# A selective scan on one Trainium2 core: GpSimd's operand instruction made over two channel blocks, and one more weighing moved to GpSimd

## The chip, the core and the metric

One core of one Trainium2 (trn2) chip runs the whole program; the other cores are idle. The metric is device microseconds of the program (us), and smaller is better. A core has five engines that each run their own instruction stream in order: PE (TensorE, matmul and transpose), DVE (VectorE), ACT (ScalarE), POOL (GpSimd) and SP (SyncE, which here only issues DMAs). They wait for each other by semaphores. SBUF is the working memory, PSUM the small memory that PE writes its results to.

## What is computed

A layer with two parts. The first is a bidirectional selective scan (two Mamba blocks, forward and backward in time), the second a mixture of eight experts with two chosen per token plus a shared expert. The input x is 2 batches x 2048 tokens x 256 channels, all in float32. The change lies in the first part. Cut to what matters:

```python
def _mamba(x, W_in, W_conv, b_conv, W_x, W_dt, b_dt, A_log, Dp, W_out):
    xp, z = split(x @ W_in.T)                       # 512 inner channels each
    xc = silu(causal_depthwise_conv(xp) + b_conv)
    dt, Bm, Cm = split(xc @ W_x.T, [16, 32])        # Bm, Cm: 16 states each
    dt = softplus(dt @ W_dt.T + b_dt)
    A = -exp(A_log)                                 # 512 x 16
    def step(h, (dt_t, u_t, B_t, C_t)):             # over time
        h = h * exp(dt_t[:, :, None] * A) + (dt_t * u_t)[:, :, None] * B_t[:, None, :]
        return h, einsum('bdn,bn->bd', h, C_t)
    y = scan(step) + xc * Dp
    return (y * silu(z)) @ W_out.T
```

So for every channel d and state n there is a recurrence over time. Its decay is exp(dt[d] A[d,n]). Its operand is (dt u)[d] B[n]; that product is what the changed instruction computes. Its result h is weighed with C[n] and summed over the 16 states.

## The kernel before

**Tiles.** Time is cut into 16 chunks (2 directions x 2 batches x 4 pieces of 512 tokens), run one after the other. A chunk has 512 channels in four blocks d of 128 partitions, and 16 states in eight groups g of NG = 2. A **step** is one channel block with one state group: a tile of 128 partitions x 2 states x 512 tokens. The steps of a chunk run over pairs p of blocks (0,1 and 2,3), inside that over g, inside that over the two blocks of the pair, so a chunk has SPC = 32 steps k = 0..31. Even k is the even block of a pair and odd k the odd one; two neighbours share B and C. `s` counts steps over all chunks, 512 in all.

**What a step does.**
- `load_b`, `load_c`: SP broadcasts two rows of B and of C to 128 partitions (3 and 4 buffers).
- `inputs` (L452): POOL multiplies du = dt u by B into `db`, one instruction of 128x1024 to a step. `db` has NDB = 10 buffers of one step.
- `decays` (L471): ACT writes the two decays `da` into PSUM banks that alternate between even and odd steps.
- `scans` (L485): DVE runs two scan instructions of 128x512.
- `weigh_own` (L491): DVE multiplies h by C, two instructions of 128x512; or, for the steps that `on_pool` names, `weigh` (L496): POOL does it in one instruction of 128x1024. For POOL the scan writes h to an SBUF tile `h` of 3 buffers, otherwise in place to PSUM.
- `carry` (L502, L506): ACT keeps the last column of h for the next chunk.
- `sums` (L518): PE transposes the weighed tile and adds it up in PSUM.
- `gate_y` (L536): after step 15 and step 31, DVE multiplies the sum by the gate.

In chunks 1 to 15 four **turned** steps (k = 6, 7, 18, 19) get their operand from PE instead of POOL; their `db` buffer holds the decay. `on_pool` names, in these chunks, the odd steps except k = 13 and 29, and also k = 4 and 16: sixteen of 32.

**The order is written out by hand.** The scheduler is off (`manual_schedule`), so each engine runs its instructions in the order in which the code emits them. In iteration s of the loop at L843 the order is: `load_b` (even s), `weigh(s-2)`, `load_c` (even s), `inputs(s+3)`, `carry(s-1)`, a softplus part at k = 20, 22, 24 and 26, `gate_y(s-5)`, `scans(s)`, `weigh_own(s)`, `decays(s+1)`, the turned operands of s+1, then the PSUM evacuations left over from the step before, `sums(s-4)`, and at last `visit(i, k)`. The last one places pieces of the neighbouring chunks' other work at fixed k (L545 to L569). Those that matter below: at k = 10 and 12 `scaled` (transposes that ACT evacuates at L372), at k = 11 `project` (evacuated by DVE at L421), at k = 12 `silu_inner` of the next chunk (L278, ACT: table load, 128x2048 silu, table load L212), at k = 13 and 15 `gated`, at k = 14 `dbc` of the next chunk (PE L289, evacuated by ACT at L294). These pieces share two PSUM banks (tag "mm"), so a third one waits until the first is evacuated. `du` itself (L342, POOL, 128x512) is made at k = 21, 23 and, in the next chunk, k = 0, 2.

Before the loop the same `db` buffers hold the input x and its normalised copy (`load_x`, `norms`).

Of the kernel before, what the change touches and what calls it, by code (L numbers as in the profile page):

```python
# [8 lines left out]
F32 = mybir.dt.float32  # L9
AF = mybir.ActivationFunctionType  # L10
ALU = mybir.AluOpType
# [4 lines left out]
P = 128  # L16
NB, T, C = 2, 2048, 256
# [6 lines left out]
TC = 512  # L24
NTC = T // TC
JC = TC // P
NG = 2
NGR = NS // NG
# [12 lines left out]
def kernel(  # L41
# [4 lines left out]
    nc = tc.nc  # L46
# [11 lines left out]
        out=flip, in_=flip, compare_op=ALU.not_equal, fill=1.0,  # L58
# [17 lines left out]
    def bc(ap, n):  # L76

        return ap.unsqueeze(1).to_broadcast([ap.shape[0], n, ap.shape[1]])

    def tiled(ap):  # L80

        return ap.rearrange("(j p) c -> p j c", p=P)
# [51 lines left out]
    with tc.tile_pool(name="mw", bufs=1) as mw, tc.tile_pool(name="mw2", bufs=2) as mw2, \  # L134
# [36 lines left out]
        def make_conv(r, n):  # L171

            w, (d, k) = weights[r], divmod(n, 4)
            if n == 0:
# [4 lines left out]
        weights, state, ready, xns, accs = {}, {}, {}, {}, {}  # L179
        chunks = [(r, b, t) for r in range(2) for b in range(NB) for t in range(NTC)]  # L180
        NCH = len(chunks)
        SPC = NP * NGR * 2
        steps = [(i, p, g, 2 * p + e) for i in range(NCH) for p in range(NP) for g in range(NGR)
                 for e in range(2)]
        NST = len(steps)
        NDB = 10
# [3 lines left out]
        def turned_step(s):  # L190
            i, p, g, _ = steps[s]
            return i > 0 and g == TURNED[p]

        def on_pool(s):

            i, _, g, d = steps[s]
            if i == 0:
                return d % 2 == 1 and g not in (NGR - 4, NGR - 2)
            return s % SPC in (4, 16) or d % 2 == 1 and g != NGR - 2

        def tokens(r, t):
            return t if r == 0 else NTC - 1 - t
# [227 lines left out]
        live = {}  # L430
# [15 lines left out]
            live["C", n] = v  # L446

        def inputs(s):
            i, _, g, d = steps[s]
            db = m2.tile([P, NG, TC], F32, tag="db", bufs=NDB, name=f"db{s}")  # L450
            if not turned_step(s):
                nc.gpsimd.tensor_tensor(db, bc(ready[i]["du"][:, d, :], NG), live["B", s // 2], ALU.mult)  # L452
            live["db", s] = db

        def operands(s):

# [36 lines left out]
        def weigh(s):  # L493
            _, _, g, d = steps[s]
            if on_pool(s):
                nc.gpsimd.tensor_tensor(live["db", s], live.pop(("h", s)), live["C", s // 2], ALU.mult)  # L496
# [107 lines left out]
        def new_stats(name):  # L604
            return {k: m2.tile([P, JC, n], F32, tag=f"n_{k}", name=f"{k}_{name}")
                    for k, n in (("st", 6), ("mv", 2), ("ve", 1), ("y", 1), ("t", 1), ("mr", 1))}

        def stats(v, src):
            for j in range(JC):
                nc.vector.bn_stats(out=v["st"][:, j, :], in_=src[:, j, :])  # L610
                nc.vector.bn_aggr(out=v["mv"][:, j, :], in_=v["st"][:, j, :])

        def rsqrt_start(v):

            y = v["y"].rearrange("p j o -> p (j o)")
            nc.scalar.activation(y, v["mv"][:, :, 1], AF.Ln, bias=eps)
            nc.scalar.activation(y, y, AF.Exp, scale=-0.5)

        def rsqrt_end(v):
            ve, y, t, mr = (v[k].rearrange("p j o -> p (j o)") for k in ("ve", "y", "t", "mr"))  # L620
            nc.vector.tensor_scalar(ve, v["mv"][:, :, 1], EPS, None, ALU.add)
            nc.vector.scalar_tensor_tensor(t, y, -0.5, y, ALU.mult, ALU.mult)
            nc.vector.tensor_tensor(t, t, ve, ALU.mult)
            nc.vector.scalar_tensor_tensor(y, t, 1.5, y, ALU.add, ALU.mult)
            nc.vector.scalar_tensor_tensor(mr, v["mv"][:, :, 0], -1.0, y, ALU.mult, ALU.mult)

        def normalize(out, v, src):
            for j in range(JC):
                nc.scalar.activation(out[:, j, :], src[:, j, :], AF.Identity,
                                     scale=v["y"][:, j, :], bias=v["mr"][:, j, :])  # L630

        def load_x(b, q):
            xt = m2.tile([P, JC, C], F32, tag="db", bufs=NDB, name=f"xt{b}_{q}")
            nc.sync.dma_start(out=xt, in_=tiled(x[b, q * TC:(q + 1) * TC, :]))
            return xt

        def norms(b, q, xt, xn):

            u = f"{b}_{q}"
            v = new_stats(f"a{u}")  # L640
            stats(v, xt)
            rsqrt_start(v)
            yield
            rsqrt_end(v)
            normalize(xt, v, xt)
            yield
            nc.vector.tensor_tensor(xt, xt, bc(mds[b][:, 1, :], JC), ALU.mult)
            nc.vector.tensor_tensor(xt, xt, bc(mds[b][:, 0, :], JC), ALU.add)
            nc.sync.dma_start(out=tiled(acc_d[b][q]), in_=xt)
            v = new_stats(f"b{u}")  # L650
            stats(v, xt)
            rsqrt_start(v)
            yield
            rsqrt_end(v)
            if xn is None:
                xn = m2.tile([P, JC, C], F32, tag="db", bufs=NDB, name=f"xo{u}")
            normalize(xn, v, xt)
            nc.sync.dma_start(out=tiled(xn_d[b][q]), in_=xn)

# [5 lines left out]
        xts = {(0, 0): load_x(0, 0)}  # L665
# [8 lines left out]
        make_rates(0)  # L674
        for n in range(4 * ND):
            make_conv(0, n)
        front = norms(0, 0, xts[0, 0], xns[0])
        next(front)
        next(front)
        for q in range(1, 3):  # L680
# [36 lines left out]
        def others():  # L717

            todo = [(0, 1), (0, 2), (0, 3), (1, 0), (1, 1)]
            live = []  # L720
            while todo or live:
                while todo and len(live) < 2:
                    k = todo.pop(0)
                    live.append(norms(*k, xts.pop(k), None))
                    if len(todo) > 1:
                        xts[todo[1]] = load_x(*todo[1])
                for g in list(live):
                    if next(g, 0) == 0:
                        live.remove(g)
                    yield  # L730
# [15 lines left out]
        for f, d in order:  # L746
            settle(False)
            e = f(0, d)
# [7 lines left out]
        for f, *d in ((dbc,), (delta, 0), (delta, 1), (delta, 2), (delta, 3)):  # L756
            settle(False)
            e = f(0, *d)
# [12 lines left out]
        for d in range(2):  # L771
            softplus_in(0, d, 1)
            softplus_out(0, d)
            input_(0, d)
        for s in range(3):
            inputs(s)
        decays(0)
        settle(False)
# [64 lines left out]
        for s in range(NST + 4 + SPC):  # L843
            i, k = divmod(s, SPC)
            if s % 2 == 0:
                if s // 2 + 3 < NST // 2:
                    load_b(s // 2 + 3)
            if 0 <= s - 2 < NST:
                weigh(s - 2)
            if s % 2 == 0 and s // 2 + 2 < NST // 2:  # L850
                load_c(s // 2 + 2)
            if s + 3 < NST:
                inputs(s + 3)
            smooth = (i + 1, soft[k]) if k in soft and i + 1 < NCH else None
            if i == 0 and k in first_soft:
                smooth = (0, first_soft[k])
            if 0 <= s - 1 < NST:
                carry(s - 1)
            if smooth:
                softplus_in(*smooth, s + 1)  # L860
                settle(False)
            if s == NST:
                open_front(0)
            if 0 <= s - 5 < NST:
                gate_y(s - 5)
            if s == NST + 5:
                open_front(0)
            if s < NST:
                scans(s)
            if smooth:  # L870
                softplus_out(*smooth)
            if s < NST:
                weigh_own(s)
            if s + 1 < NST:
                decays(s + 1)
                operands(s + 1)
            settle(False)
            settle(True)
            next(late, None)
            if 0 <= s - 4 < NST:  # L880
                sums(s - 4)
            if i == NCH - 1 and k in early_loads:
                early_loads[k][0](*early_loads[k][1:])
            if i == NCH and k in (10, 13, 14, 23):
                open_front({10: 0, 13: 1, 14: 0, 23: 1}[k])
            if i < NCH + 1:
                visit(i, k)
                if s == 8:
                    silu_gate(0)
                if k == 8 and 2 <= i < 2 + NB:  # L890
                    nc.sync.dma_start(out=xs_d[i - 2].rearrange("(p n) (m f) -> p (n m) f", p=P, f=P),
                                      in_=bc(ident, NTS * TS // P * 2))
            if i + 2 < NCH and chunks[i + 2][0] != chunks[i + 1][0]:
                r = chunks[i + 2][0]
                if k == 2:
                    fetch_weights(r)
                if 12 <= k < 12 + 4 * ND:
                    make_conv(r, k - 12)
                if k == 8:
                    make_rates(r)  # L900
                if k == 21:
                    fetch_dt(r)
                if k == 26:
                    fetch_in(r)
            if 0 < i < NCH and k == 24 and "out" not in weights[chunks[i][0]]:
                fetch_out(chunks[i][0])
# [500 lines left out]
```

## Time and profile before

Three runs gave a median of 2440.74 us (2439.56 to 2442.28). The profile comes from one further execution:

| what | value |
|---|---|
| the profiled execution's own time | 2438.82 us |
| its span, first to last instruction | 2436.9 us |
| mean granted TensorE clock | 0.895 of full |
| busy share: PE / DVE / ACT / POOL | 81% / 83% / 67% / 76% |
| POOL operands, L452 | 452 instructions, 2368 ns each |
| POOL weighing, L496 | 252 instructions, 2371 ns each |
| DVE scans, L485 | 1024 instructions in four groups, some 1.26 us each |
| DVE weighing, L491, h in `da` banks | 460 instructions, 676 ns each |

How to read it: a span of an instruction can overlap the next one's by some ten ns, so the sum over a row is a little above the time that the row takes; where it matters, the spacing from one start to the next is used. The loop over the chunks runs from about 105 us to 1896 us. The steady chunks (from about 760 us to 1780 us) repeat every 109.2 us: the first turned scan of a chunk starts at 1160.74, 1269.96, 1379.18, 1488.41 us. The expert part follows, from about 1900 us to the end, and is not touched.

### The profile page before, as it was taken

The page shows a single profiled execution, that of the slowest core. Times are in us where ns is not written, and L with a number is a line of the kernel's source. Part 1 is how long each engine was busy: PE and PEld are TensorE (multiplying, and loading weights), DVE is VectorE, ACT ScalarE, POOL GpSimd, SP SyncE. Part 2 cuts the span into 40 slices and gives each one's busy share as a digit, 9 for nine tenths or more (in the row PEclk, how much of TensorE's full clock was granted, in tenths as well). Part 3 has the DMA queues.
Part 4 walks back from the last instruction along what each step waited for, and adds up shares of the span by engine and source line. Part 5 has one row for each costly group of instructions (what it writes and reads, how often), then busy time and mean ns, then how long its engine had stood idle before and what let it go on. Part 6 is the DMA issues. An engine that isn't in the chain of part 4 may idle for free. (4 is left out here: it accounts for less than half of the span.)

```text
span 2436.9 us, 30322 instructions
## 1 busy us (share of the span) xinstructions
PE 1985.9 (81%) x9512; PEld 1369.4 (56%) x9512; DVE 2022.9 (83%) x2691; ACT 1621.1 (67%) x3375; POOL 1858.0 (76%) x979
## 2 busy tenths in 40 slices
PE   6366879797888878797888878797856698899997
PEld 2143545565655555565655545565546464788884
DVE  5499998999999999999999999999999675432333
ACT  5557786877778787877778787877765224354331
POOL 0367998989999999999999999999999205041305
PEclk9677888798989988898989988898977898999999
DMA  5344447484454454454454444444446312387873
GB/s 166 108 153 157 147 157 237 166 256 156 165 168 154 157 181 149 166 170 169 150 171 157 159 162 139 171 168 157 149 168 220 104 31 97 115 259 241 268 235 115
DMA packets 239974, 403.08 MB, mean 165 GB/s; under 512 B 38818, under 2 KB 171938, under 8 KB 239812
## 3 DMA queue, kind: packets, MB, share of 16 engines
q1 hardware_dynamic: 220724, 370.72, 46.5%
q0 software_dynamic: 6144, 16.79, 2.0%
q10 hardware_dynamic: 12944, 13.64, 1.6%
q8 instruction: 75, 1.23, 0.2%
q14 instruction: 87, 0.71, 0.1%
HBM read 346.54 MB, written 54.53 MB: 165 GB/s over the span
## 5 line engine op out<-in xcount | busy, mean ns | idle before, releaser
L452 POOL TENSOR_TENSOR db<-du,B 128x1024 f32<-128x1024 f32 x452 | 1061.5, 2368 | 14.2 <-DMA B<-bcs 14.1
L496 POOL TENSOR_TENSOR db<-h,C 128x1024 f32<-128x1024 f32 x252 | 597.5, 2371 | 67.5 <-issue 54.8
L471 ACT ACTIVATE da<-dt,w_a 128x512 f32<-128x512 f32 x904 | 594.7, 688 | 76.1 <-DVE dt L336 46.0
L518 PE MATMUL y<-ident,db 128*128 128x128 f32 x4096 | 570.1, 288 | 36.6 <-POOL db L496 34.0
L518 PEld LDWEIGHTS y<-ident,db 128*128 128x128 f32 x4096 | 506.6, 150 | 157.9 <-issue 102.1
L485 DVE TENSOR_TENSOR_SCAN da<-da,hl,db 128x512 f32<-128x512 f32 x460 | 562.9, 1269 | 4.9 <-POOL db L452 3.7
L485 DVE TENSOR_TENSOR_SCAN h<-da,hl,db 128x512 f32<-128x512 f32 x444 | 540.2, 1263 | 16.6 <-ACT da L471 16.4
L491 DVE TENSOR_TENSOR db<-da,C 128x512 f32<-128x512 f32 x460 | 292.2, 676 | 17.7 <-DMA C<-bcs 9.7
L272 PE MATMUL psc<-xp,w_conv 128*128 128x512 f32 x512 | 234.3, 601 | 9.4 <-ACT xp L261 6.4
L255 PE MATMUL psx<-xT,w_in 128*128 128x512 f32 x256 | 156.0, 730 | 100.2 <-ACT hl L506 86.8
L1104 POOL DMA_INDIRECT xs<-xs,slot x64 | 62.8, 981 | 203.5 <-ACT xs L1100 194.3
L390 PE MATMUL psz<-w_in,xT 128*128 128x512 f32 x256 | 149.3, 716 | 55.7 <-ACT bT L353 33.9
L1234 POOL DMA_INDIRECT two<-ys,slot x64 | 62.4, 974 | 159.7 <-DMA ys<-yo 64.3
L342 POOL TENSOR_TENSOR du<-dt,xc 128x512 f32<-128x512 f32 x64 | 81.5, 1274 | 98.9 <-DVE dt L336 98.9
L289 PE MATMUL psd<-xc,w_x 128*48 128x512 f32 x128 | 100.5, 959 | 67.5 <-ACT hl L506 47.6
L272 PEld LDWEIGHTS psc<-xp,w_conv 128*128 128x128 f32 x512 | 93.5, 192 | 106.7 <-issue 95.5
L418 PE MATMUL pso<-w_out,yg 128*128 128x256 f32 x512 | 118.5, 385 | 23.8 <-ACT e L312 22.6
L255 PEld LDWEIGHTS psx<-xT,w_in 128*128 128x128 f32 x256 | 50.0, 224 | 155.3 <-ACT hl L506 109.4
L1125 PE MATMUL pg<-fxT,s 128*128 128x512 f32 x256 | 120.1, 624 | 4.3 <-ACT hs L1130 4.0
L1180 DVE COPY gT<-qgT 128x512 f32<-128x512 f32 x46 | 31.8, 691 | 107.8 <-PE qgT L931 107.7
L506 ACT COPY hl<-da 128x1 f32<-128x1 f32 x460 | 61.7, 157 | 84.7 <-DVE db L491 82.1
L418 PEld LDWEIGHTS pso<-w_out,yg 128*128 128x128 f32 x512 | 95.6, 192 | 39.3 <-ACT e L312 25.6
(218 smaller groups left out, 3154.1 us busy)
## 6 DMA issues: line engine op xcount, KB each, us to landing
C<-bcs SPq DMA_DIRECT2D x256, 512.0 KB, 4.4
B<-bcs SPq DMA_DIRECT2D x226, 512.0 KB, 4.1
we<-in_w_dram SPq DMA_DIRECT2D x138, 256.0 KB, 3.7
acc<-acc SPq DMA_DIRECT2D x32, 512.0 KB, 5.2
xs<-ident SPq DMA_DIRECT2D x2, 5888.0 KB, 24.0
xg<-xs SPq DMA_DIRECT2D x46, 256.0 KB, 3.8
ys<-yo ACTq DMA_DIRECT2D x46, 256.0 KB, 3.0
xn<-xn SPq DMA_DIRECT2D x16, 512.0 KB, 5.8
```

The costliest lines, as they stand in the source:

```text
L255: nc.tensor.matmul(ps, w["in"][:, k, d * P:(d + 1) * P], v["xT"][:, k, :], start=(k == 0), stop=(k == KC - 1))
L272: nc.tensor.matmul(ps, w["conv"][:, d, k, :], v["xp"][:, d, k:k + TC], start=(k == 0), stop=(k == 3))
L289: nc.tensor.matmul(ps[:RK + 2 * NS, :], w["x"][:, d, :], v["xc"][:, d, :], start=(d == 0), stop=(d == ND - 1))
L390: nc.tensor.matmul(ps, v["xT"][:, k, j * P:(j + 1) * P], w["in"][:, k, DI:2 * DI], start=(k == 0), stop=(k == KC - 1))
L418: nc.tensor.matmul(ps[:, n, :], v["yg"][:, d, n * P:(n + 1) * P], wo[:, d, :], start=(d == 0), stop=(d == ND - 1))
L452: nc.gpsimd.tensor_tensor(db, bc(ready[i]["du"][:, d, :], NG), live["B", s // 2], ALU.mult)
L471: nc.scalar.activation(da[n], ready[i]["dt"][:, d, :], AF.Exp, scale=w["a"][:, d, m:m + 1])
L485: nc.vector.tensor_tensor_scan(h[n], da[n], x[n], hl[:, d, m:m + 1], ALU.mult, ALU.add)
L491: nc.vector.tensor_tensor(live["db", s][:, n, :], h, live["C", s // 2][:, n, :], ALU.mult)
L496: nc.gpsimd.tensor_tensor(live["db", s], live.pop(("h", s)), live["C", s // 2], ALU.mult)
L518: nc.tensor.matmul(ys["y"][j // 2][:, j % 2, d % 2 * P:(d % 2 + 1) * P], src[:, j * P:(j + 1) * P], ident, is_transpose=True, start=(first ...
L1125: nc.tensor.matmul(ps, s12[:, n, k, m * P:(m + 1) * P], xTs[b, q][:, k, :], start=(k == 0), stop=(k == KC - 1))
```

## The change

`inputs` is called once for two steps (every odd s, and before the loop for steps 0 and 2), and makes the operands of both channel blocks with one instruction of 128x2048. It reads du of blocks d and d+1, each repeated for the two states, and B, repeated for the two blocks. `db` becomes five buffers of two steps, so the bytes are the same. Turned steps take a buffer as before, without the instruction. `on_pool` names k = 13 too in chunks 1 to 15. Before the loop, x and its normalised copy share one double buffer.

```diff
-            return s % SPC in (4, 16) or d % 2 == 1 and g != NGR - 2
+            return s % SPC in (4, 16, 13) or d % 2 == 1 and g != NGR - 2
...
         def inputs(s):
-            i, _, g, d = steps[s]
-            db = m2.tile([P, NG, TC], F32, tag="db", bufs=NDB, name=f"db{s}")
+
+            i, p, _, d = steps[s]
+            db = m2.tile([P, 2, NG, TC], F32, tag="db", bufs=NDB // 2, name=f"db{s}")
             if not turned_step(s):
-                nc.gpsimd.tensor_tensor(db, bc(ready[i]["du"][:, d, :], NG), live["B", s // 2], ALU.mult)
-            live["db", s] = db
+                nc.gpsimd.tensor_tensor(
+                    db, ready[i]["du"][:, d:d + 2, :].unsqueeze(2).to_broadcast([P, 2, NG, TC]),
+                    live["B", s // 2].unsqueeze(1).to_broadcast([P, 2, NG, TC]), ALU.mult)
+            for e in range(2):
+                live["db", s + e] = db[:, e, :, :]
...
         def load_x(b, q):
-            xt = m2.tile([P, JC, C], F32, tag="db", bufs=NDB, name=f"xt{b}_{q}")
-            nc.sync.dma_start(out=xt, in_=tiled(x[b, q * TC:(q + 1) * TC, :]))
-            return xt
+            xt = m2.tile([P, 2, JC, C], F32, tag="db", bufs=NDB // 2, name=f"xt{b}_{q}")
+            nc.sync.dma_start(out=xt[:, 0, :, :], in_=tiled(x[b, q * TC:(q + 1) * TC, :]))
+            return xt[:, 0, :, :], xt[:, 1, :, :]
...
-        for s in range(3):
+        for s in (0, 2):
             inputs(s)
...
-            if s + 3 < NST:
+            if s % 2 == 1 and s + 3 < NST:
                 inputs(s + 3)
```

On POOL, odd iterations now hold `weigh(s-2)`, then the operands of s+3 and s+4 in one; even iterations hold at most a weighing. The order on the other engines is the same but for step 13's weighing and carry.

More of the change, by code (lines that the diff above doesn't have):

```diff
@@ L654, in norms @@
             rsqrt_end(v)
-            if xn is None:
-                xn = m2.tile([P, JC, C], F32, tag="db", bufs=NDB, name=f"xo{u}")
             normalize(xn, v, xt)
@@ L676 @@
             make_conv(0, n)
-        front = norms(0, 0, xts[0, 0], xns[0])
+        front = norms(0, 0, xts[0, 0][0], xns[0])
         next(front)
@@ L723, in others @@
                     k = todo.pop(0)
-                    live.append(norms(*k, xts.pop(k), None))
+                    live.append(norms(*k, *xts.pop(k)))
                     if len(todo) > 1:
```

## The prediction

> **What bounds the kernel now.** I read the page's busy shares first, then the stages, then the waits of DVE and POOL in the steady chunks (815 to 1735 us, 8.4 chunks), and last the timelines of one chunk. The page's first part:
>
> ```profile
> PE 1985.9 (81%) x9512; PEld 1369.4 (56%) x9512; DVE 2022.9 (83%) x2691; ACT 1621.1 (67%) x3375; POOL 1858.0 (76%) x979
> ```
>
> These are averages over two parts of the program. In the steady chunks DVE is busy 112 of every 115 us and POOL 113, so both look like the bound, and the change gives to both. What each still waits for tells more (engine, line, releaser: us in total, times, longest):
>
> ```profile
> POOL db L496 <- issue: 10.6, 9, 1.2
> POOL db L496 <- POOL db L452: 6.8, 8, 0.9
> DVE h L485 <- ACT da L471: 10.6, 8, 1.7
> DVE op L485 <- issue: 8.3, 16, 0.8
> ```
>
> POOL stands idle twice in a chunk, 1.2 us and 0.9 us, both times before a weighing: at steps 3 and 15 it has caught up with DVE and must wait for the scan. DVE waits once in every chunk for a decay of ACT, some 1.3 us, always at step 17, and 0.8 us at step 6 and 0.2 us at step 18 for a turned operand of PE. So neither is a bound by itself. What sets step 17? ACT's timeline in chunk 7 (start, us, line):
>
> ```profile
> 957.98 0.16 ACT L506 COPY hl<-da 128x1 f32<-128x1 f32 x1 [0.42 <-DVE db L491]
> 958.03 1.31 ACT L471 ACTIVATE da<-dt,w_a 128x512 f32<-128x512 f32 x2
> ...
> 963.42 1.91 ACT L278 ACTIVATE xc<-xc 128x2048 f32<-128x2048 f32 x1
> ...
> 966.84 1.30 ACT L471 ACTIVATE da<-dt,w_a 128x512 f32<-128x512 f32 x2
> 968.08 1.55 ACT L372 ACTIVATE ab<-psu,bT 128x256 f32<-128x256 f32 x4
> ...
> 976.07 0.58 ACT L294 COPY xd<-psd 48x512 f32<-48x512 f32 x1 [3.13 <-PE psd L289]
> 976.55 0.20 ACT L502 COPY hl<-h 128x2 f32<-128x2 f32 x1
> 976.65 1.30 ACT L471 ACTIVATE da<-dt,w_a 128x512 f32<-128x512 f32 x2
> ```
>
> ```profile
> 969.68 6.35 PE L289 MATMUL psd<-xc,w_x 128*48 128x512 f32 x8 [3.66 <-ACT hl L506]
> ```
>
> The chain starts at 957.98, when DVE ends its weighing of step 10. From there to 969.5 ACT works without a gap: decays of step 12, the evacuation L372, decays of 13, a table load, the silu, a table load, decays of 14, L372 again. That last evacuation frees the bank for `dbc`, whose matmuls then take 6.35 us. Only then can ACT evacuate them (L294) and make the decays of step 17. On DVE:
>
> ```profile
> 966.72 1.27 DVE L491 TENSOR_TENSOR db<-da,C 128x512 f32<-128x512 f32 x2
> 967.90 2.46 DVE L485 TENSOR_TENSOR_SCAN da<-da,hl,db 128x512 f32<-128x512 f32 x2
> ...
> 977.44 2.46 DVE L485 TENSOR_TENSOR_SCAN h<-da,hl,db 128x512 f32<-128x512 f32 x2 [1.18 <-ACT da L471]
> ```
>
> The first row is step 13's weighing, the one that the change takes from DVE. It lies inside the stretch from 957.98 to 977.44 in which ACT and PE, not DVE, set the end. So a chunk's period of 109.2 us is: DVE from step 17 to the weighing of step 10, then 19.5 us of ACT, PE, ACT.
>
> **Part 1: DVE loses a weighing at step 13, chunks 1 to 15.** 966.72 to 967.90 is 1.18 us, in 15 chunks 17.7 us. What of it shortens the path? In steps 11 to 17 DVE's end is set by the chain, so the wait at step 17 grows from 1.2 to 2.4 us in all, and step 17 starts when it did. Part of the new wait comes earlier: DVE is free for step 14 at 966.72, but that step's first decay is ready at 966.84 + 0.67 = 967.5. The same holds in chunks 1 and 5 to 14 (waits of 1.2 to 1.7 us at that place). In chunk 4 the matmuls took 5.33 us and the wait is only 0.16 us, but it is there. In chunks 2 and 3 step 14's weighing waits 5.67 and 4.05 us for C from a DMA, which comes no earlier. So in chunks 1 to 14 the gain is **0**. In chunk 15 there is no next chunk, no silu and no `dbc`; DVE has no wait above 0.2 us there, and 1.18 us would count, if POOL lets it. ACT saves a copy (two of L506 against one of L502, some 0.1 us) behind the evacuation that frees the bank, off the chain: 0.
>
> **Part 2: POOL's instruction of two steps.** Spacing of starts in one stretch of POOL's timeline:
>
> ```profile
> 992.65 2.35 POOL L452 TENSOR_TENSOR db<-du,B 128x1024 f32<-128x1024 f32 x1
> 994.97 1.26 POOL L342 TENSOR_TENSOR du<-dt,xc 128x512 f32<-128x512 f32 x1
> 996.19 2.36 POOL L452 TENSOR_TENSOR db<-du,B 128x1024 f32<-128x1024 f32 x1
> ```
>
> 128x1024 takes 2.32 us, 128x512 takes 1.22. That is 1.10 per 512 elements and 0.12 fixed, so 128x2048 should take 0.12 + 4 x 1.10 = **4.52 us** against 4.64 for two: 0.12 saved. No row shows such a pattern (two operands repeated, three free dimensions). Its ends are 4.40, if even the fixed part goes, and 4 x 1.22 = 4.88, if it were worked off in rows of 512 that each pay it. I take 4.52: a repeated operand costs nothing (medians 2.365 for L452, 2.363 for L496 without), and neither do more, shorter rows (L1277, 128x1024 in four rows of 256: 2.33 us). The Trainium skill ("GPSIMD Engine Reference", section 3.1) measured 4497 ns for such an instruction of 2048 floats; by it the sum below would be 0.2 us lower.
>
> POOL's work in a steady chunk is now 28 x 2.32 + 16 x 2.32 + 4 x 1.22 = 107.0 us; it becomes 14 x 4.52 + 17 x 2.32 + 4.9 = **107.6 us**. The period is 109.2, so 1.6 of the 2.2 us of idle time stay. Cost 0, if the operands still come in time.
>
> **Do they?** The first step of a pair now gets its operand only when both are done, some 2.2 us later, and behind step 13 POOL is 2.32 us later. From the weighing of step 3 (936.24 in chunk 7, where POOL waits for DVE) I add up the new order: pair 10/11 is ready at 952.2, DVE's step 10 starts at 954.32; pair 12/13 at 959.1 against 960.22; pair 14/15 at 965.9 against 967.5; pair 16/17 at 972.8 against 973.4; pair 20/21 at 981.9 against 987.19. All in time, and a delay in steps 12 to 16 would only use the 2.4 us that DVE waits anyway. POOL comes back to the next weighing of step 3 with 1.1 us to spare (1043.9 against 1045.03), du of k = 2 no later than now. The waits that the change adds elsewhere: PE's `sums(13)` waits for POOL, done at 975.1, and PE comes there at 980.27. SP's C load at k = 16 waits for the same weighing (975.1 instead of 967.9), lands 4.4 us later and is needed at 991.60; the B load queued behind it is needed later still. The h buffer of step 17 is now that of step 13: free at 975.1, needed at 977.44. At the start the first scan comes 2.2 us later than 104.90, and then waits for C until 115.29 as now: 0.
>
> **Where POOL is late.** (a) Chunk 4. POOL lost 6.30 and 5.30 us to B loads in chunks 2 and 3 and has no idle time until 755 us. Its operand of step 17 ended at 647.4; with one weighing more and 15 pairs it ends at 647.4 + 2.32 - 1.8 = 647.9, step 13's weighing at 650.2, and step 17, which needs its buffer, started at 649.91: **+0.3 us**. (b) Chunk 15, where DVE has no softplus, no chain, and POOL is the slower engine. POOL's rows, and DVE's step 28:
>
> ```profile
> 1809.50 2.37 POOL L496 TENSOR_TENSOR db<-h,C 128x1024 f32<-128x1024 f32 x1 [1.29 <-issue]
> ...
> 1879.09 4.71 POOL L452 TENSOR_TENSOR db<-du,B 128x1024 f32<-128x1024 f32 x2
> 1883.73 2.38 POOL L496 TENSOR_TENSOR db<-h,C 128x1024 f32<-128x1024 f32 x1
> ```
>
> ```profile
> 1882.45 2.44 DVE L485 TENSOR_TENSOR_SCAN da<-da,hl,db 128x512 f32<-128x512 f32 x2
> ```
>
> The operand of step 28 was ready at 1881.4, 1.0 us before its use; that of step 29 at 1883.73. After the change both come with the pair. From 1809.50 on there is one weighing more and ten pairs: 1883.73 + 2.32 - 1.2 = 1884.9. Step 28 starts there instead of 1882.45: **+2.4 us**. Pair 30/31 (1891.7) then meets DVE at 1892.0, so nothing is added. The scans end at 1897.9 instead of 1895.45, and the expert part, which begins with DVE's work behind them, moves along.
>
> A rule of the skill speaks against longer POOL instructions, and the row comes first: beside POOL, DVE's L92 (both inputs in SBUF) took 3.27 us, ending with POOL's 3.20 us instruction, against 1.23 alone; at 151 to 160 us four tiny DVE instructions took 1.7 to 2.4 us each, each ending with a POOL instruction. The skill's "GPSIMD Engine Reference", section 1, says that GpSimd shares its SBUF interfaces with VectorE when that has two SBUF inputs. By it, a longer POOL instruction could hold such DVE instructions twice as long. The loop's DVE instructions all take one input from PSUM (scans 1249 to 1292 ns throughout), and in chunk 0 POOL runs dry at 159.6 us either way: 0.
>
> **Sum.** 0.3 + 2.4 = +2.7 us on the profiled execution's 2438.82 us gives 2441.5. That execution is 1.9 us under the median of the runs, 2440.74, so the forecast is **2443.5 us**. With 4.40 a pair it is 1.2 us less (2442); with 4.64 POOL's chunk is 109.3 us, its reserve is gone, (a) and (b) grow by 1.8 and 1.2 us and step 10 comes up to 1 us late once: 2447 to 2449. A measurement of this kernel tells 0.2% (4.9 us) from no change.
>
> **Rivals.**
> *POOL becomes the bound (slower).* Place: the weighing of step 3, where POOL has 1.1 us to spare. Point: 14 pairs + 44.3 us = 109.2, so a pair above 4.63 us. Price: 14 us in each of 14 chunks for each us above, and the 4 us of chunk 15: at 4.70, 2440.7 + 14 + 4 = 2459; at 4.88, 2440.7 + 49 + 6 = 2496. For it: two repeated operands and three dimensions are unseen. Against: repeats and rows cost nothing in the rows above. 0.32.
> *The weighing counts after all (faster).* If the chain were shorter than I read it, DVE's 1.18 us would come off 14 chunks: 2440.7 - 16.5 + 2.7 = 2427. Against: the wait for ACT stands in every chunk, and even at 5.33 us of matmul. 0.10.
> *Buffers of two steps hold POOL up (the change doesn't save).* Pair 20/21 needs `sums(11)`, which PE ends at 977.0, behind `dbc`; POOL comes at 977.4. A late PE would use up POOL's 1.1 us, and cost nothing: 2443 to 2445. 0.06. The forecast as it stands has 0.52.
>
> **Numbers.** Slower by over 0.2% (above 2445.6) is the first rival, 0.32; faster is the second, 0.10; the rest is 0.58. The range reaches from 2436 to 2458: it leaves out most of the second rival (0.08) and the first with pairs above 4.70 (0.12).
>
> **What would show it.** Right: 226 operand instructions of 4.5 us; the period stays 109.2 us; DVE's waits for `da` in steps 14 to 17 grow from 1.3 to 2.4 us a chunk; POOL's idle time before step 15's weighing goes, that before step 3's stays near 1 us; in chunk 15 DVE waits for `db` of POOL some 3.6 us in all. Wrong: a period below 108.5 (the chain isn't rigid), or no idle time of POOL in the steady chunks and DVE waiting for `db` there (POOL is the bound).

## The result, and the profile after

The changed kernel takes 2444.02 us (median of 20 runs, 2439.49 to 2448.55) against 2437.86 us of the kernel before on the same chip (20 runs, 2435.71 to 2442.28): a ratio of 1.0022 (of the means), 95% interval 1.0015 to 1.0029. That is 6 us more, where 2.7 us were forecast; the interval lies above 1, so it is slower, by little. The profiled execution took 2446.37 us, span 2444.7 us, mean granted TensorE clock 0.898.

The costliest groups of the changed kernel, POOL's two kinds (busy us, mean ns of one, idle time just before and its main releaser):

```profile
L453 POOL TENSOR_TENSOR db<-du,B 128x2048 f32<-128x2048 f32 x226 | 1026.2, 4544 | 16.6 <-DMA B<-bcs 16.1
L500 POOL TENSOR_TENSOR db<-h,C 128x1024 f32<-128x1024 f32 x267 | 629.6, 2366 | 72.1 <-issue 60.2
```

226 instructions of two steps, 15 weighings more. In POOL's timeline the two-step instruction takes 4.50 us from start to start. DVE's waits in eight steady chunks (815 to 1735 us; total, times, longest):

```profile
DVE h L489 <- ACT da L475: 12.6, 8, 1.7
DVE op L489 <- issue: 8.4, 16, 0.8
DVE da L489 <- issue: 6.8, 8, 1.1
```

The `da` rows are steps 17 and 14. Before there was only the first, with 10.6 us, or 1.3 a chunk; now there are 19.4 us, 2.4 a chunk. All that DVE saved became waiting. The same place in DVE's and in PE's timeline of one chunk:

```profile
1383.80 2.46 DVE L489 TENSOR_TENSOR_SCAN op<-db,hl,op 128x512 f32<-128x512 f32 x2 [0.74 <-issue]
1408.90 2.47 DVE L489 TENSOR_TENSOR_SCAN da<-da,hl,db 128x512 f32<-128x512 f32 x2 [0.82 <-issue]
```

```profile
1410.96 6.47 PE L289 MATMUL psd<-xc,w_x 128*48 128x512 f32 x8 [3.65 <-ACT ab L372]
```

The first row is step 6; the next chunk's starts at 1493.03, 109.2 us later, as before. The second is step 14, which now waits for its decay. The third names the releaser of `dbc`: ACT's evacuation L372, the one that the forecast put at the end of ACT's gapless stretch.

ACT's two decays for step 14 start at 1408.12 (1.30 us in all), and POOL's pair for steps 14 and 15 ended at 1407.0, so it is the decay that step 14 waits for.

So the steady chunks lost nothing, and the time came in at three other places. By the start of step 6, the changed kernel is 2.0 us behind in chunk 1, 0.7 us ahead in chunk 3, 3.3 behind in chunk 4, 4.5 in chunk 5, a constant 4.6 from chunk 8 to 14, and 6.8 at the end of the scans (1902.29 against 1895.45). Two looks at the kernel before differ by 1.4 us there, so only the larger steps mean something. The 2.7 us that came back between chunk 1 and chunk 3 (5.0 in the run a1 below, 4.2 in a3, 0.4 in a second look at the kernel before) are explained by no run.

**Chunk 0.** DVE's norm of the input, in the changed kernel, and POOL beside it:

```profile
191.61 3.42 DVE L651 TENSOR_TENSOR xt<-xt,md 128x1024 f32<-128x1024 f32 x1
195.06 5.40 DVE L652 TENSOR_TENSOR xt<-xt,md 128x1024 f32<-128x1024 f32 x1
```

```profile
191.59 2.36 POOL L500 TENSOR_TENSOR db<-h,C 128x1024 f32<-128x1024 f32 x1 [6.68 <-issue]
193.91 5.47 POOL L453 TENSOR_TENSOR db<-du,B 128x2048 f32<-128x2048 f32 x1
```

The same place in the kernel before, where the norm is L647 and L648:

```profile
193.25 1.23 DVE L647 TENSOR_TENSOR xt<-xt,md 128x1024 f32<-128x1024 f32 x1
194.51 3.26 DVE L648 TENSOR_TENSOR xt<-xt,md 128x1024 f32<-128x1024 f32 x1
```

```profile
193.67 3.01 POOL L496 TENSOR_TENSOR db<-h,C 128x1024 f32<-128x1024 f32 x1 [7.20 <-issue]
```

The DVE rows have two SBUF inputs; before, these two took 1.23 and 3.26 us. Add up the ends. POOL's weighing ends at 193.95 and L651, started 0.02 us after it, at 195.03, 1.08 later. POOL's pair ends at 199.38 and L652 at 200.46, again 1.08 later. So each DVE instruction stands still until POOL's is done and then takes its own 1.1 us. Before, L647 (the same norm) started 0.4 us ahead of POOL's weighing and ran in 1.23 us, the weighing then took 3.01 us, and L648 waited for the rest of it. So there are two losses: 2.2 us at L651, where POOL now comes first, and 2.1 us at L652, where the instruction in the way is twice as long.

**Chunk 3.** SP's queue in the changed kernel:

```profile
509.82 0.32 SPq L444 DMA_DIRECT2D C<-bcs  x1
510.19 0.54 SPq L893 DMA_DIRECT2D xs<-ident  x1
514.32 16.47 SPq L438 DMA_DIRECT2D B<-bcs  x1
```

The C load waits for a buffer that POOL's weighing of a step frees: POOL's row has two weighings from 505.07 for 4.72 us, so the end is 509.79, and the load goes at 509.82. Behind it stand a store and a B load that sits 16 us in the queue, and behind that the C of step 14. Counted from step 6 the C load is issued 5.8 us later, against 4.5 before, and C is there after 34.45 us, against 31.91. DVE's wait for it is 6.88 us instead of 4.05.

**Chunk 15.** DVE's waits for POOL in the timeline of the changed kernel, two of five:

```profile
1882.47 2.47 DVE L489 TENSOR_TENSOR_SCAN da<-da,hl,db 128x512 f32<-128x512 f32 x2 [0.78 <-POOL db L453]
1889.26 2.47 DVE L489 TENSOR_TENSOR_SCAN da<-da,hl,db 128x512 f32<-128x512 f32 x2 [0.78 <-POOL db L453]
```

Together 2.9 us from 1850 on, at steps 17, 22, 24, 26 and 28, where 3.6 were forecast.

### The profile page after: what moved, and what is told of

It is laid out like the page before. It is cut to its first block, busy times and chain, and to the rows that moved or that the text cites. A ratio compares the mean times of both kernels' runs of the same rounds, so it can differ in the third digit from the quotient of the medians.

```text
span 2444.7 us, 29699 instructions
## 1 busy us (share of the span) xinstructions
PE 1981.6 (81%) x9512; PEld 1367.1 (56%) x9512; DVE 2010.3 (82%) x2661; ACT 1619.6 (66%) x3360; POOL 1859.0 (76%) x768
## 3 DMA queue, kind: packets, MB, share of 16 engines
q8 instruction: 75, 1.23, 0.2%
## 5 line engine op out<-in xcount | busy, mean ns | idle before, releaser
L453 POOL TENSOR_TENSOR db<-du,B 128x2048 f32<-128x2048 f32 x226 | 1026.2, 4544 | 16.6 <-DMA B<-bcs 16.1
L500 POOL TENSOR_TENSOR db<-h,C 128x1024 f32<-128x1024 f32 x267 | 629.6, 2366 | 72.1 <-issue 60.2
L489 DVE TENSOR_TENSOR_SCAN h<-da,hl,db 128x512 f32<-128x512 f32 x474 | 577.0, 1264 | 21.0 <-ACT da L475 20.4
L489 DVE TENSOR_TENSOR_SCAN da<-da,hl,db 128x512 f32<-128x512 f32 x430 | 526.2, 1269 | 21.2 <-issue 11.7
L495 DVE TENSOR_TENSOR db<-da,C 128x512 f32<-128x512 f32 x430 | 273.2, 676 | 18.1 <-DMA C<-bcs 12.8
```

Source lines behind the costliest of these rows:

```text
L453: nc.gpsimd.tensor_tensor(db, ready[i]["du"][:, d:d + 2, :].unsqueeze(2).to_broadcast([P, 2, NG, TC]), live["B", s // 2].unsqueeze(1).to_b ...
L489: nc.vector.tensor_tensor_scan(h[n], da[n], x[n], hl[:, d, m:m + 1], ALU.mult, ALU.add)
L495: nc.vector.tensor_tensor(live["db", s][:, n, :], h, live["C", s // 2][:, n, :], ALU.mult)
```

## The experiments

All in one table, by the starts of the gate product of step 15 in the profiles (chunk 0's; the mean period over the eight chunks up to chunk 14's; the time from chunk 14's to the end of the scans), with the ratio to the kernel before on the same chip. The runs a1 to a4 were made on a chip on which the expert part takes some 60 us longer (604 to 609 us behind the scans, against 541 to 545 on the others); of the kernel before there is no profile there, so what they say of the scans is compared with the other chips' profiles.

| run | chunk 0's gate | period | chunk 14's gate to end | end of scans | ratio (95%) |
|---|---|---|---|---|---|
| before | 213.2 | 109.21 | 145.0 | 1895.5 | 1 |
| b0_before | 212.5 | 109.24 | 145.0 | 1894.1 | one look, 2439.93 us |
| changed | 215.9 | 109.21 | 147.2 | 1902.3 | 1.0022 (1.0015 to 1.0029) |
| a1_pair_only | 216.4 | 109.24 | 145.7 | 1896.2 | 1.0021 (1.0008 to 1.0033) |
| a2_w13_only | 211.6 | 109.12 | 148.7 | 1901.1 | 1.0042 (1.0025 to 1.0058) |
| a3_single0 | 211.9 | 109.21 | 147.1 | 1897.2 | 1.0016 (1.0003 to 1.0029) |
| a4_w29 | 216.0 | 109.19 | 145.3 | 1898.7 | 1.0031 (1.0020 to 1.0042) |
| b1_skip29 | 211.3 | 109.21 | 143.8 | 1893.2 | 1.0000 (0.9990 to 1.0009) |
| b2_skip22 | 211.3 | 107.64 | 143.8 | 1875.6 | 0.9926 (0.9909 to 0.9942) |
| b3_w22s | 212.3 | 108.35 | 148.6 | 1893.1 | 0.9987 (0.9977 to 0.9996) |
| c1_swap_16_22 | 212.2 | 107.79 | 143.8 | 1879.8 | 0.9939 (0.9925 to 0.9952) |
| c2_pair_swap | 212.3 | 108.01 | 144.5 | 1878.8 | 0.9951 (0.9937 to 0.9965) |
| c3_pair_8_22 | 212.6 | 107.48 | 144.5 | 1872.3 | 0.9913 (0.9899 to 0.9926) |
| c4_pair_22_24 | 212.4 | 108.28 | 147.2 | 1885.6 | 0.9962 (0.9948 to 0.9975) |

**The change taken apart.** a1 is the changed kernel without its `on_pool` edit:

```diff
-            return s % SPC in (4, 16, 13) or d % 2 == 1 and g != NGR - 2
+            return s % SPC in (4, 16) or d % 2 == 1 and g != NGR - 2
```

> The changed kernel with step 13's weighing left on DVE: only the pairing of POOL's operand instructions (226 of 128x2048 in place of 452 of 128x1024). Theory (the pairing costs in chunk 0 alone, where the longer POOL instructions hold up DVE's L651 and L652, +4.4 us; POOL late in chunk 15 comes from the weighing): chunk period 109.2 us, chunk 15 within 0.5 us of before, all in all about +4 us over before, ratio 1.0010 to 1.0020. Rival A (the weighing that was moved costs the time, not the pairing): within 1 us of before. Rival B (pairs make operands late in every chunk): period above 109.3 us and the time as with the whole change or above.

The period stays and chunk 0 is as in the changed kernel (216.4), so in chunk 0 the pairs cost and the moved weighing does not. But chunk 0's loss doesn't all arrive: by the start of step 6, a1 is 3.3 us behind the first profile of before in chunk 1 and level with it from chunk 8 on, and its scans end 0.7 to 2.1 us later than in the two profiles of before. The ratio is a little above what was expected, and it can't come from the scans alone; what is left arises behind them, and with no profile of before from that chip its cause stays open.

a2 is that one `on_pool` edit on the kernel before.

> The kernel before with step 13's weighing on POOL: only the move, operands in single instructions. Theory: chunk 0 as before (the norms L651 and L652 in 1.2 and 3.3 us); POOL's chunk is 28 x 2.32 + 17 x 2.32 + 4.9 = 109.3 us against a period of 109.2, so the period stays within 0.2 us of 109.2, and chunk 15 is about 2 to 3 us longer: +2 to +5 us over before, ratio 1.0005 to 1.0020. DVE's waits for da in steps 14 to 17 grow to about 2.4 us a chunk. Rival (DVE's weighing of step 13 counts): the period falls by up to 1.18 us, as far as POOL allows it, so to no less than 109.3: this run cannot show a gain, the runs that move or leave out a weighing can.

Chunk 0 is as before (211.6). The loss at the end is 3.7 us and not 2 to 3: without pairs POOL's 109.3 us a chunk leave it no reserve at all, and it is later when chunk 15 begins. The time missed its range on the upper side (1.0042, of which the scans show 5.6 to 7.0 us). So the pairs do pay for themselves where POOL has this much to do: the changed kernel loses 2.2 us at the end, a2 3.7. By the end of the scans the move alone costs 5.6 to 7.0 us, the pairs alone 0.7 to 2.1 and both together 6.8 to 8.2. So by these profiles, one of each, most of the loss goes with the move. What the pairs lose in chunk 0 is mostly made up behind it in a1; a3, next, says otherwise.

a3 makes chunk 0's operands singly, in the same buffers:

```diff
+                if i == 0:
+                    for e in range(2):
+                        nc.gpsimd.tensor_tensor(db[:, e, :, :], bc(ready[i]["du"][:, d + e, :], NG),
+                                                live["B", s // 2], ALU.mult)
+                else:
```

> The changed kernel, but chunk 0's operands are made by two 128x1024 instructions a pair, in the same buffers of two steps; chunks 1 to 15 as changed. Theory (the longer instruction holds up DVE's two-SBUF-input norms L651 and L652 in chunk 0): these take 1.2 and 3.3 us again, the first turned scan of chunk 1 comes some 4 us earlier than in the changed kernel, chunk 15 keeps its +2.2 us: +1 to +3 us over before, ratio 1.0004 to 1.0012. Rival (chunk 0's loss is from the buffers of two steps or the later first operand): chunk 0 stays as in the changed kernel, ratio 1.002 or above.

Its norms in DVE's timeline (lines shifted by five):

```profile
192.00 1.22 DVE L656 TENSOR_TENSOR xt<-xt,md 128x1024 f32<-128x1024 f32 x1
193.26 3.26 DVE L657 TENSOR_TENSOR xt<-xt,md 128x1024 f32<-128x1024 f32 x1
```

1.2 and 3.3 us again, and 4.0 us less than in the changed kernel at chunk 0's gate. Over all runs the three kernels with pairs in chunk 0 have this gate at 215.9 to 216.4, the eleven others at 211.3 to 213.2. So the buffers of two steps cost nothing. The later first operand (the first scan starts at 106.51 in the changed kernel, at 104.64 here) costs nothing either, since DVE waits for C until 114.30 and 114.50 behind it. At the end of the scans 5.1 us are gained against the changed kernel, more than a1 leaves for chunk 0; the times (1.0016 here, 1.0022 of the changed kernel elsewhere, intervals of 0.0026 and 0.0014) can't tell the two apart.

**Is it only step 13 whose weighing is worth nothing?** a4 moves step 29 instead, `in (4, 16, 29)`.

> The changed kernel with step 29's weighing on POOL in place of step 13's: the same amount of work moved, but from the part of the chunk between step 17 and step 10 of the next, in which the trace shows DVE without a wait. Theory (a weighing counts only outside the stretch that ACT and PE set): the period falls from 109.2 us to between 108.0 and 108.8 (POOL's own chunk of 107.6 is the floor); with chunk 0's +4.4 and chunk 15's +2 the time is 2 to 12 us below the kernel before, ratio 0.995 to 0.9995. Rival (DVE is not what sets the period there, or POOL already is): period 109.2 us and the time of the changed kernel.

This failed: 109.19 us, no gain. DVE's waits in one chunk of a4, and ACT's and POOL's rows at the first of them:

```profile
1357.53 2.47 DVE L489 TENSOR_TENSOR_SCAN da<-da,hl,db 128x512 f32<-128x512 f32 x2 [0.95 <-issue]
1382.08 2.46 DVE L489 TENSOR_TENSOR_SCAN op<-db,hl,op 128x512 f32<-128x512 f32 x2 [0.85 <-issue]
```

```profile
1355.26 1.28 ACT L212 ACT_TABLE_LOAD   x1
...
1356.75 1.30 ACT L475 ACTIVATE da<-dt,w_a 128x512 f32<-128x512 f32 x2
```

```profile
1345.56 4.53 POOL L453 TENSOR_TENSOR db<-du,B 128x2048 f32<-128x2048 f32 x1
```

The first is step 30. Its operand was ready: POOL's pair for steps 30 and 31 ended at 1350.09. Its decays were not: ACT makes them behind the gate's silu and a table load, from 1356.75 on, and the scan starts 0.78 us after that. So ACT takes back 0.95 of the 1.18 us at once. The run b1 below, which has no pairs, shows the same: step 30 waits 0.94 us and starts 0.78 us after ACT's row.

```profile
1353.50 2.47 DVE L485 TENSOR_TENSOR_SCAN da<-da,hl,db 128x512 f32<-128x512 f32 x2 [0.94 <-issue]
```

```profile
1352.72 1.30 ACT L471 ACTIVATE da<-dt,w_a 128x512 f32<-128x512 f32 x2
```

(The expectation of c2 below still takes this wait for one on POOL's pairs.) The second is step 6, which waits in the kernel before too (0.74 us, there as here with no releaser shown). The forecast saw this wait, put it down to a turned operand of PE, and drew nothing from it. It is the end of a second stretch, from step 27 to step 6, in which DVE doesn't set the end. In the kernel before, ACT goes without a longer gap from 1347.80 through the gate's silu with two table loads to the second L245 at 1357.14; PE's rows show what comes of it:

```profile
1355.87 4.16 PE L255 MATMUL psx<-xT,w_in 128*128 128x512 f32 x4 [5.79 <-ACT hl L506]
...
1378.49 1.04 PE L208 MATMUL op<-ident,ab 128*128 128x128 f32 x8
```

From the first row PE works on without a gap to 1383, through the projections and convolutions. The second row, in that queue, is the operand of step 6, which starts at 1379.18. So the refined theory was: a weighing is worth its 1.18 us only between step 17 and step 27 and between step 6 and step 10. Two runs leave one weighing out, on the kernel before, to take POOL out of the question (b1 step 29, as here; b2 step 22):

```diff
-            if not on_pool(s):
+            if not on_pool(s) and (s < SPC or s % SPC != 29):
```

b0:

> The kernel before, looked at once more beside the others, since its time differs between chips. Expected of it by every theory: a chunk period of 109.2 us and the end of the scans at 1895 to 1897 us, as in the first profile; a longer time comes from the expert part behind the scans alone, where the weights come by DMA.

b1:

> The kernel before without the weighing by C of step 29 in chunks 1 to 15 (left out, neither engine does it). Refined theory (a second stretch, from step 27 to step 6 of the next chunk, is set by ACT's gate silu with its table loads and then by PE's convolutions; DVE waits 0.74 us at step 6 already): period stays 109.2 us, only chunk 15, where no such chain runs, gains 1.2 us; ratio 0.9990 to 1.0005. First theory (DVE sets the end between step 17 and step 10 throughout): period 108.0 us, 17 us less, ratio 0.993.

b2:

> The kernel before without the weighing by C of step 22 in chunks 1 to 15 (left out, neither engine does it). Refined theory (between step 17 and step 27 DVE sets the end): period 109.2 - 1.18 = 108.0 us, or 108.2 where an ACT wait of 0.2 us grows, so 14 to 18 us less, ratio 0.9925 to 0.9945. Rival (POOL or ACT sets the period by itself, and every weighing of DVE is hidden): period above 109.0 us, ratio above 0.998.

It holds. b0 is the kernel before again (its scans end at 1894.1, a little below what was expected). The same instruction left out is worth nothing at step 29 (109.21 us; chunk 15 gains 1.2) and 18 us in all at step 22. The period falls by 1.57 us, more than 1.18: the `dbc` matmuls took 3.6 to 6.6 us in these chunks, where the kernel before shows 6.3 to 6.5, so the stretch behind step 10 is not rigid either. Why they took less is not shown.

Did the faster `dbc` bring the gain, and not the weighing? DVE's starts, cut into four pieces a chunk (means over chunks 7 to 13, us; lowest to highest where they differ by over 0.2), tell the two apart:

| run | step 6 to 11 | 11 to 17 | 17 to 27 | 27 to 6 |
|---|---|---|---|---|
| before | 15.35 | 19.67 | 40.22 | 33.96 |
| b1_skip29 | 15.35 | 19.67 | 40.22 | 33.96 |
| b2_skip22 | 15.35 | 18.77 (18.31 to 19.81) | 38.93 (38.70 to 39.04) | 34.56 (34.27 to 34.80) |
| c1_swap_16_22 | 15.35 | 19.53 (19.50 to 19.71) | 38.75 (38.70 to 39.03) | 34.08 (33.60 to 34.56) |
| c3_pair_8_22 | 14.18 | 19.85 (19.50 to 20.00) | 38.92 (38.70 to 39.10) | 34.50 (34.26 to 34.62) |

`dbc` lies in the second piece. The third, with step 22, loses 1.2 to 1.5 us in every chunk, also in chunk 11 of b2, where `dbc` took 6.43 us (39.04). So the weighing counts there; the faster `dbc` adds some 0.9 us in b2, of which the last piece takes 0.6 back. In c1 (below) the second piece is 19.50 us whether `dbc` takes 3.63 or 5.07.

> The changed kernel with step 22's weighing on POOL in place of step 13's, and chunk 0's operands in single instructions. The amount of work moved is that of the change; only its place differs. Refined theory: DVE's 1.18 us count here, POOL's chunk stays at 107.6 us, so the period falls to 108.0 to 108.6 us (POOL's order around step 22 can cost part of it): 8 to 16 us less than before, ratio 0.9935 to 0.997. Rival (moving a weighing brings nothing anywhere, since POOL then sets the period or gives its operands late): period 109.2 us or more, ratio 1.0005 or more.

b3, `in (4, 16, 22)` on a3, moves as much as the change does, at a better place. The period falls as expected (107.2 to 110.2, mean 108.35), but the ratio is only 0.9987, above the range: chunk 15 costs 3.6 us, where DVE waits for POOL up to 3.10 us at a time, and from 1000 to 1735 us ACT's L274 waits up to 4.7 us for POOL's `du` (0.9 before). That points to POOL, which has hardly any idle time left. So a place where DVE counts is needed, and POOL must get something off. Step 16's weighing lies in the hidden stretch 10 to 17, and DVE can have it back for nothing. c1 does only that swap, on the kernel before:

```diff
-            return s % SPC in (4, 16) or d % 2 == 1 and g != NGR - 2
+            return s % SPC in (4, 22) or d % 2 == 1 and g != NGR - 2
```

c1:

> The kernel before, operands in single instructions, with step 22's weighing on POOL and step 16's back on DVE: no engine does more or less, only the places change. Step 16 lies in the stretch that ACT and PE set (DVE waits 1.3 us at step 17), step 22 in the one that DVE sets. Theory: 1.18 us a chunk gained at step 22, nothing lost at 16; POOL's chunk 107.0 us; period 108.0 to 108.4 us, time 10 to 17 us below before, ratio 0.993 to 0.996. Rival (only the amount on each engine counts, or POOL comes late behind step 22): period 109.2 us or more, ratio 0.999 or more.

c2:

> As the run without pairs that swaps steps 16 and 22, but with the changed kernel's pairs in chunks 1 to 15 (single instructions in chunk 0). POOL's chunk 105.3 us. Theory: period 108.0 to 108.3 us, chunk 15 no longer than before, ratio 0.993 to 0.996; against the run without pairs the pairs are worth at most what POOL waits cost there (0 to 0.4 us a chunk). Rival (the pairs hold operands up where POOL has no idle time, as beside step 29's weighing): 0.3 us a chunk or more above the run without pairs.

c3:

> As the pairs with steps 16 and 22 swapped, and steps 4 and 8 swapped too: POOL weighs 8 and 22, DVE 4 and 16. POOL's chunk is the same 105.3 us. Step 8 lies in the stretch from step 6 to step 10 that DVE sets; step 4 lies in the other stretch, where DVE waits only 0.74 us, so 0.4 us of its 1.18 are lost. Theory: period 107.2 to 107.8 us, ratio 0.987 to 0.993. Rival (POOL behind step 8 gives the operands of steps 12 and 13 late and ACT's chain starts late): period 108.0 us or more.

c4:

> As the pairs with steps 16 and 22 swapped, and steps 4 and 24 swapped too: POOL weighs 22 and 24, DVE 4 and 16. Theory: DVE's bound is 107.3 us as for 8 and 22, but POOL then has 43.5 us of work in the 40.2 us from step 17 to step 27 and must use up its lead there: period 107.3 to 108.3 us, ratio 0.987 to 0.996. Rival (POOL late there costs all): period 109.2 us or more.

c2 to c4 are a3 with `in (4, 22)`, `in (8, 22)` and `in (22, 24)`. c1 gains 16 us with no engine doing more or less; its period, 107.79, is just below the range that was given. In c2 the pairs add nothing to it (108.01 against 107.79 a chunk): POOL's 107.0 us were already enough. c3 also trades step 4 for step 8, and is the fastest: 2417.87 us, 0.9913. DVE's waits in it from 1000 to 1600 us:

```profile
DVE e L334 <- ACT sl L329: 1.4, 5, 0.3
DVE da L494 <- ACT da L480: 0.9, 3, 0.3
DVE h L494 <- ACT da L480: 0.8, 2, 0.4
```

In 5.6 chunks all its waits (six kinds, three shown) come to 4.2 us, where before they were 13.5: DVE itself is the bound now. c4 does the same to DVE but puts two weighings on POOL within three steps; its period, 108.28, is inside the range that was given, at its upper end, and POOL is late in chunk 15 (147.2), which puts the ratio just above its own range.

## Why the prediction was right, and where not

**Right.** *Part 1*: the weighing of step 13 is worth nothing in the steady chunks. The period stays at 109.2 us, and the waits for `da` grow to 2.4 us a chunk (forecast: 1.3 to 2.4). *Part 2*: 4.50 us measured, 4.52 forecast; the rival in which POOL becomes the bound above 4.63 us did not happen. *Operands in time*: no wait for `db` in the steady chunks. POOL's idle time before step 15's weighing went from 6.8 us in eight chunks to 0.3; that before step 3's stayed, 1.4 us at the longest (1.2 before). *Startup*: 0, as forecast. *Chunk 15*: +2.2 us, forecast +2.4, though spread over five steps from 17 on and not at step 28 alone; a3 has it too, a1 (0.7) hardly.

**Wrong, chunk 0.** The step "in chunk 0 POOL runs dry at 159.6 us either way: 0" looked at the tiny instructions at 151 to 160 us, which did take no longer in all (8.6 us against 8.8), and missed the norm at 191 us, where L647 and L648 stand in the profile of before at 193 us with 1.23 and 3.26 us. That POOL can hold up such instructions was even weighed there, and the sum took 0. "The loop's DVE instructions all take one input from PSUM" isn't so for this norm, and the 3.27 us row of L92 was misread: it ends not with POOL's instruction but 1.08 us behind it. Measured: 4.4 us in that stretch, of which a3 gets 4.0 back. The Trainium skill ("SBUF — State Buffer", section "SBUF: two separate sides") says that the pair of ports is an exclusive lock that the first to start holds for its whole instruction; the two ends above, each 1.08 us behind POOL's, agree. How much of it reaches the end is less sure: 5.1 us by a3 against the changed kernel, but only 0.7 to 2.1 by a1 against before. The two don't agree, and no run settles it.

**Wrong, chunk 3.** "C from a DMA, which comes no earlier" was costed at nothing; C came later, since its loads queue at SP behind one that POOL's weighing frees. The wait grew by 2.8 us. C arrives 34.0 to 34.5 us after step 6 in the changed kernel, a1, a2 and a3, 32 in both profiles of before and 30.8 in c3, where that load goes 2.6 us after step 6. In c1 and b2, where DVE is the one that got ahead, the load goes 5.9 and 5.6 us after step 6 and C comes after 34.6 and 34.8. Over all fourteen profiles C comes 27.4 to 29.2 us after that load. All of this fits, but no run was made for this queue alone. a1 (the pairs alone) and a2 (the move alone) both have the late C, so either is enough for it. *Chunk 4* was forecast at +0.3; 1.2 us were found, with `dbc` at 6.4 instead of 5.3 us. The 0.16 us wait there that Part 1 counted as the chain's is POOL's by its row (L496).

**Wrong, the picture.** That "a chunk's period of 109.2 us is: DVE from step 17 to the weighing of step 10, then 19.5 us of ACT, PE, ACT" is half of it. The 0.74 us wait at step 6, which the forecast named and left out of this sum, ends a second such stretch, of 31.6 us from the end of step 27's scan. It didn't touch this forecast, since step 13 lies in the first; it spoiled the expectation of a4.

So the sum of 2.7 us was too small by 3.5 to 4 (6.8 us by the scans' ends in the profiles, 6.2 by the medians). That 2443.5 lies so near to 2444.02 has a second reason: the kernel before, run 20 times beside it, took 2437.86 us, 2.9 less than the median that the forecast started from. That the steady chunks neither gain nor lose was forecast for the right reason; that the number fits so well is partly luck.

## What to carry to other kernels

Before work is moved from one engine to another, mark on the timeline which engine sets the end in each stretch of the period: here each small wait of the busiest engine, 0.7 and 1.2 us, closed a stretch in which its work was free. The same 1.18 us was worth nothing at steps 13 and 29, and 1.2 to 1.5 us a chunk at step 22; swapping two weighings between such stretches gained 16 us with no work saved. And when an instruction of POOL gets longer, look for DVE instructions with two SBUF inputs beside it, in the first chunk and the last as well as in the steady ones.

## What the chip showed beside

- A DVE instruction of 128x1024 with two SBUF inputs, 1.23 us alone, took 3.3 to 3.4 us behind a POOL instruction of 1024 elements and 5.4 us behind one of 2048; POOL pays the same way when DVE is first (the pair's 4.5 became 5.47 us, a weighing's 2.36 became 3.01, in a3 3.38). POOL was 0.02 us ahead at 191.6 us in the changed kernel, and DVE waited; DVE was 0.06 us ahead in a3, and POOL waited.
- A DVE instruction with one SBUF input can be held too: L625 of the changed kernel (TENSOR_SCALAR, 128x4) took 3.60 us at 149.57, to the end of POOL's pair, against 0.16 us elsewhere. BATCH_NORM_STATS2 beside a pair at 181 to 183 us took 0.39 us as always.
- POOL's two-input instruction costs almost by elements alone: 128x2048 with both operands repeated takes 4.50 us, two of 128x1024 with one repeated take 4.64.
- The same kernel took 2497.56 us on one chip and 2437.86 to 2439.64 on the others. In the four profiles from the first chip the expert part is some 60 us longer, and in the four busiest slices of their pages (61 to 63 us each) DMA moved 194 to 243 GB/s, where the other pages show 235 to 268. Whether DMA is the cause was not tested.
